# Cross-attention on one core: the second batch's queries from seven half-width products in place of eight

## The chip, the cores and the metric

The kernel runs on one core of a Trainium2 chip. Its engines work in parallel, each through its own list of instructions and in that list's order: TensorE (PE) multiplies matrices, VectorE (DVE) reduces, adds and transposes, ScalarE (ACT) copies and takes exponentials, GpSimd (POOL) does elementwise work, and SyncE (SP) issues nearly all DMAs. They meet at semaphores. The metric is device time in microseconds (us); lower is better. Three runs of the kernel before gave 497.66, 497.72 and 498.04 us, so its median is 497.72.

## The reference, cut to what matters

`x` is (2, 2048, 640), the context is (2, 154, 1024), all in f32; 20 heads of 32. The first 77 rows of the context are text, the other 77 are image prompts, each with its own keys, values and softmax.

```python
q    = split(x @ Wq.T)
k, v = split(text @ Wk.T), split(text @ Wv.T)
ki, vi = split(ip @ Wk_ip.T), split(ip @ Wv_ip.T)
out  = softmax(q k' / sqrt(32)) v + softmax(q ki' / sqrt(32)) vi
return merge(out) @ Wo.T + bo + x
```

## The kernel before, in words

Everything is transposed, with channels on the 128 partitions: 640 channels are 5 chunks of 128 (4 heads each), and the 2048 tokens of a batch are 4 blocks of 512. A *unit* `u` is half a batch's tokens (1024, two blocks `h`) of one chunk; there are 20 units, the first ten of batch 0. Two units make a chunk `q` of a batch (0 to 9).

Work on a unit: `queries` multiplies one token block by one chunk of Wq (5 matmuls of 512 columns, one per chunk of contracted channels), and `take_queries` copies the result out of PSUM, scaled by 1/sqrt(32). The unit's eight tiles of 128 tokens form three groups `s` of 3, 3 and 2 tiles. For each group `scores` (R) multiplies queries by keys into one *half* of PSUM, four banks of the eight, one bank per head; `take` (K, on ACT) copies the scores into the buffer `pb`; `maxima` (M, DVE); `subtract` (S, POOL); `exponential` (E, ACT); `sums` (D, DVE); `invert` (I, DVE); `normalise` (N, POOL); `transpose` (T, DVE). When both units of a chunk are through, `attend` (A, PE) multiplies by the values, and CA copies its result to `aT`.

Three tables of (unit, group) give other softmax forms. A BIASED group subtracts its maxima inside the exponential (one ACT instruction for each row of 77, so no S on POOL), a DIRECT group does so straight from PSUM (no K, and its banks stay taken until E is done), and a SUMMED group also lets ACT sum the rows (no D on DVE, and a read of the accumulator on ACT behind each exponential).

The output projection of batch 0 is done with seven block products in place of eight (`product`, m and cm in the list, with the token differences G of `sum_t` on POOL and the weight sums W). That of batch 1 is the tail of the kernel: weight sums V, token sums X, 66 products F and their sums Y into the output, with `last_chunk` for the fifth chunk (p, z, yz).

What sets the order is a list of words written out by hand or by a program, `SCHEDULE`. Each word emits one step, `@n` names its bank or half, and since every engine runs its own instructions in the order of emission, the list sets the order on all engines at once, SP's DMAs included: LX loads a token block of batch 1, LQ a chunk of Wq, VS spreads values, SF and SS fetch and store batch 0's output, and LA loads what batch 1's outputs are added to.

In batch 1, before the change, each (chunk, block) is loaded anew (20 LX words) into a ring of three blocks, and its queries are made by `queries`: 20 groups of 5 matmuls in this batch.

## Time and profile before

| what | value |
|---|---|
| median of three runs | 497.72 us |
| span of the profiled execution | 496.7 us |
| PE busy | 490.3 us (99%) |
| DVE busy | 408.5 us (82%) |
| POOL busy | 362.5 us (73%) |
| ACT busy | 315.0 us (63%) |
| bytes moved by DMA | 69.38 MB |
| granted TensorE clock | 1.000 |

A busy time is the time in which at least one instruction of the engine was under way. Matmuls overlap, so the mean duration of one (601 ns for 512 columns) is more than the distance from one to the next; the distance is read from the starts in the timeline. An f32 matmul of the source shows as two MATMUL records. The chain of waits follows the last instruction back to the first. The profiled execution's span is 1.0 us below the median of the runs.

### The profile page before, as it was taken

The page shows a single profiled execution, that of the slowest core. Times are in us where ns is not written, and L with a number is a line of the kernel's source. Part 1 is how long each engine was busy: PE and PEld are TensorE (multiplying, and loading weights), DVE is VectorE, ACT ScalarE, POOL GpSimd, SP SyncE. Part 2 cuts the span into 40 slices and gives each one's busy share as a digit, 9 for nine tenths or more (in the row PEclk, how much of TensorE's full clock was granted, in tenths as well). Part 3 has the DMA queues.
Part 4 walks back from the last instruction along what each step waited for, and adds up shares of the span by engine and source line. Part 5 has one row for each costly group of instructions (what it writes and reads, how often), then busy time and mean ns, then how long its engine had stood idle before and what let it go on. Part 6 is the DMA issues. An engine that isn't in the chain of part 4 may idle for free.

```text
span 496.7 us, 10482 instructions
## 1 busy us (share of the span) xinstructions
PE 490.3 (99%) x4114; PEld 287.9 (58%) x4114; DVE 408.5 (82%) x412; ACT 315.0 (63%) x1021; POOL 362.5 (73%) x157
## 2 busy tenths in 40 slices
PE   8999999999999999999999999999999999999997
PEld 5676657657547556456647654755755675444442
DVE  0069989979979989969976896687999978898877
ACT  1165878978978778668999786587578966100000
POOL 0069978798888999989874858565899888284830
PEclk9999999999999999999999999999999999999999
DMA  8991440332360454886445177418525401420115
GB/s 259 356 246 40 132 120 1 106 93 69 92 213 3 132 178 132 274 273 237 158 152 191 58 244 210 133 57 246 174 69 171 127 23 43 149 84 1 43 73 223
DMA packets 67474, 69.38 MB, mean 140 GB/s; under 512 B 5473, under 2 KB 47201, under 8 KB 67425
## 3 DMA queue, kind: packets, MB, share of 16 engines
q1 hardware_dynamic: 66704, 68.00, 43.8%
q8 instruction: 32, 0.52, 0.5%
q10 hardware_dynamic: 720, 0.72, 0.4%
q14 instruction: 18, 0.14, 0.1%
HBM read 54.94 MB, written 10.49 MB: 132 GB/s over the span
## 4 chain that ended last, share of the span: by engine, by line
PE 92%; DMA 3%; SPq 1%; DVE 1%; POOL 1%; ACT 1%; issue 0%; POOLq 0%
PE bank L201 33%; PE bank L848 11%; PE bank L490 10%; PE bank L233 10%; PE bank L332 10%; PE bank L142 9%; PE bank L471 6%; PE bank L500 3%; DMA aT<-in_L_xattn_Wk_ip_dram 2%; DMA wq<-in_L_xattn_Wq_dram 2%; SPq L534 1%; POOL pb L316 1%; DVE den L306 0%; ACT pb L301 0%; SPq L132 0%
## 5 line engine op out<-in xcount | busy, mean ns | idle before, releaser
L316 POOL TENSOR_TENSOR pb<-pb,rden 128x1848 f32<-128x1848 f32 (+1 forms) x60 | 176.1, 2944 | 39.7 <-DVE rden L311 35.5
L201 PE MATMUL bank<-x,wq 128*128 128x512 f32 x400 | 180.4, 601 | 0.6 <-DMA x<-in_x_dram 0.5
L295 POOL TENSOR_TENSOR pb<-pb,mx 128x1848 f32<-128x1848 f32 (+1 forms) x38 | 119.3, 3152 | 51.8 <-DVE mx L281 51.5
L201 PEld LDWEIGHTS bank<-x,wq 128*128 128x128 f32 x400 | 74.1, 191 | 86.7 <-issue 80.8
L323 DVE STREAM_TRANSPOSE pb<-pb 128x1920 f32<-128x1920 f32 (+1 forms) x60 | 115.7, 1932 | 4.9 <-POOL pb L316 4.3
L281 DVE TENSOR_REDUCE mx<-pb 128x24 f32<-128x1848 f32 (+1 forms) x51 | 93.7, 1850 | 30.7 <-ACT pb L245 30.5
L245 ACT COPY pb<-bank 128x462 f32<-128x462 f32 (+1 forms) x204 | 87.2, 539 | 36.0 <-PE bank L233 35.4
L306 DVE TENSOR_REDUCE den<-pb 128x24 f32<-128x1848 f32 (+1 forms) x47 | 88.7, 1895 | 17.6 <-ACT pb L301 13.3
L301 ACT ACTIVATE pb<-pb 128x1848 f32<-128x1848 f32 (+1 forms) x38 | 64.2, 1696 | 17.8 <-POOL pb L295 17.5
L269 ACT ACTIVATE pb<-pb,mx 128x77 f32<-128x77 f32 x224 | 67.8, 364 | 0.3 <-DVE mx L281 0.2
L233 PEld LDWEIGHTS bank<-kT,qT 32*128 32x128 f32 x1280 | 45.4, 184 | 26.9 <-issue 15.6
L269 ACT ACTIVATE pb<-bank,mx 128x77 f32<-128x77 f32 x184 | 51.8, 386 | 9.3 <-DVE mx L284 9.3
L233 PE MATMUL bank<-kT,qT 32*128 32x154 f32 x1280 | 56.2, 305 | 0.3 <-ACT kT L559 0.3
L332 PE MATMUL bank<-pb,v 32*32 32x512 f32 x1600 | 55.2, 597 | 0.0
L142 PE MATMUL bank<-wo_ct,aT 128*128 128x154 f32 x320 | 45.6, 296 | 0.3 <-DMA aT<-in_L_xattn_Wk_ip_dram 0.3
L142 PEld LDWEIGHTS bank<-wo_ct,aT 128*128 128x128 f32 x320 | 42.9, 188 | 3.6 <-issue 2.2
L332 PEld LDWEIGHTS bank<-pb,v 32*32 32x32 f32 x1600 | 29.9, 103 | 22.8 <-issue 10.7
L211 ACT ACTIVATE qT<-bank 128x512 f32<-128x512 f32 x40 | 24.2, 619 | 22.1 <-PE bank L201 22.0
L471 PE MATMUL bank<-aT,wo_ct 128*128 128x512 f32 x80 | 36.1, 596 | 0.0
L269 ACT ACTIVATION_READ_ACCUMULATOR pb<-bank,mx 128x1 f32 x128 | 33.6, 267 | 0.0
L490 PE MATMUL bank<-aT,wo_ct 128*128 128x256 f32 x128 | 32.3, 385 | 0.0
L490 PEld LDWEIGHTS bank<-aT,wo_ct 128*128 128x128 f32 x128 | 23.7, 190 | 6.5 <-issue 3.0
(75 smaller groups left out, 434.4 us busy)
## 6 DMA issues: line engine op xcount, KB each, us to landing
x<-in_x_dram SPq DMA_DIRECT2D x20, 1280.0 KB, 6.7
out_dram<-acc SPq DMA_DIRECT2D x20, 256.0 KB, 2.3
x<-in_x_dram SPq DMA_DIRECT2D x18, 256.0 KB, 5.9
acc<-in_x_dram SPq DMA_DIRECT2D x16, 256.0 KB, 4.7
out_dram<-x SPq DMA_DIRECT2D x15, 256.0 KB, 2.0
v<-vS SPq DMA_DIRECT2D x160, 20.0 KB, 2.8
wq<-in_L_xattn_Wq_dram SPq DMA_DIRECT2D x9, 320.0 KB, 5.0
aT<-in_L_xattn_Wk_dram SPq DMA_DIRECT2D x5, 512.0 KB, 5.5
```

Of the source, the lines that this page charges most:

```text
L142: nc.tensor.matmul(keys_in(out), loaded[n][:, k, :], cT[:, k, :, t, :], start=(k == 0), stop=(k == NCC - 1))
L201: nc.tensor.matmul(pq, wqs[q % 3][:, k, :], xs[place_of(u, h)][:, k, :], start=(k == 0), stop=(k == NC - 1),)
L233: nc.tensor.matmul(ps[g][:, ts(t, 2 * L)], qTs[(u, h)][g * D : (g + 1) * D, ts(st, P)], kT[g * D : (g + 1) * D, c, b].rearrange("p t l -> ...
L245: nc.scalar.copy(keys_of(u, s)[:, :, g], ps[g][:, : n * 2 * L].rearrange("p (n l) -> p n l", n=n))
L269: nc.scalar.activation(row, row if ps is None else rows_in(ps[g], n)[:, t, x], AF.Exp, bias=maxs[(u, s)][:, *one], accum_out=None if den i ...
L281: nc.vector.tensor_reduce(mx, rows_of(u, s), AX.X, ALU.max, negate=negate)
L295: nc.gpsimd.tensor_tensor(rows_of(u, s), rows_of(u, s), maxs[(u, s)].unsqueeze(3).to_broadcast([P, n, 2, L]), ALU.subtract)
L306: nc.vector.tensor_reduce(den_of(u, s), rows_of(u, s), AX.X, ALU.add)
L316: nc.gpsimd.tensor_tensor(rows_of(u, s), rows_of(u, s), rdens[(u, s)].unsqueeze(3).to_broadcast([P, n, 2, L]), ALU.mult)
L323: nc.vector.transpose(p, p)
L332: nc.tensor.matmul(pa[r][g * D : (g + 1) * D, :], v4s[q % 2][rows, g, k, :], zones[rows, :, g, k, :], start=(k == 0), stop=(k == NK - 1),)
L490: nc.tensor.matmul(part, w_of[m][:, kp, op], t_of(m, b, i)[:, kp], start=(op == kp == 0 and m in (1, 2, 5)), stop=(op == 1 and kp == 1 and ...
```

## The change

1. Batch 1's chunks are taken in pairs: chunks 0 and 1 (`p` = 0), 2 and 3 (`p` = 1). For each pair and each token block `i`, the first four channel chunks form a 2x2 block product: two output chunks by two pairs of input chunks, and two halves of 256 tokens. It is computed from seven products `q_product` (words g) of 2 matmuls of 256 columns; the fifth input chunk is added to four of them with one more matmul of 256 columns. `take_q_product` (words t) puts the results into the query tiles: products 1, 4, 5 and 6 by a copy on ACT, 2, 3 and 7 by an add or subtract on DVE. Product 6 goes on accumulating in the bank of product 1, then 7, then 4; product 3 goes on in that of 5.
2. The token sums (`sum_x`, words U, four per pair and block) are written into the token blocks themselves and one spare place; 24 are on POOL and 8 on DVE. The weight sums (`sum_wq`, words Z, six per pair) are on POOL.
3. Token blocks of batch 1 are loaded for a pair: 12 LX words, into a ring of two blocks (`RING`). The third block that batch 0 leaves (`SPARE`) holds two more query tiles, the spare token sum and the weight sums. LA now loads the output's tokens into it as well, ahead of the other two loads.
4. The scale 1/sqrt(32) moves from the queries to the keys. Query tiles come from a list kept by hand (`new_q`, `used_q`) in place of a pool.
5. The three tables of softmax forms are new: DIRECT has 7 groups in place of 9, BIASED 15 in place of 13, SUMMED 8 in place of 13. Groups that need S on POOL are still 38, of which 12 in place of 5 are groups of two tiles.
6. SCHEDULE is written anew.

```diff
-        (11, 0), (13, 0), (13, 2), (14, 0), (14, 2), (15, 1), (15, 2), (16, 2), (18, 1),
+        (3, 2), (7, 1), (11, 0), (11, 2), (13, 0), (13, 2), (15, 1),
...
-    qpool = ctx.enter_context(tc.tile_pool(name="qpool", bufs=5))
+    q_slots = [const.tile([P, TB], F32, name=f"qs_{n}") for n in range(QS)]
...
-        return late.index((u, h)) % XROOM if b else sub * NH + h
+        return late.index((first_of(u), h)) % RING if b else sub * NH + h
...
-        nc.scalar.mul(qT, pq, SCALE)
+        nc.scalar.copy(new_q(u, h), pq)
...
+    def sum_x(p, i, n, eng):
+        x, y = {
+            1: lambda: (x_part(p, i, 0, 0), x_part(p, i, 0, 1)),
+            2: lambda: (x_sum(p, i, 1), x_part(p, i, 1, 1)),
+            3: lambda: (x_part(p, i, 0, 1), x_part(p, i, 1, 1)),
+            4: lambda: (x_sum(p, i, 2), x_part(p, i, 1, 0)),
+        }[n]()
+        eng.tensor_tensor(x_sum(p, i, n), x, y, ALU.add)
...
+    def q_product(p, i, m, ps):
+        w = {
+            1: lambda: wq_part(p, 0, 0), 2: lambda: wq_part(p, 0, 1), 4: lambda: wq_part(p, 1, 1),
+        }.get(m, lambda: wq_sum(p, m))()
...
+        part = ps[:, :HT]
+        for kp in range(2):
+            nc.tensor.matmul(
+                part, w[:, kp], x[:, kp], start=(kp == 0 and m in (1, 2, 5)), stop=(kp == 1 and not fifth),
+                skip_group_check=True,
+            )
+        if fifth:
...
+            nc.tensor.matmul(part, w5, five, start=False, stop=True, skip_group_check=True)
+    def take_q_product(p, i, m, ps):
...
+        if m in (2, 3, 7):
+            nc.vector.tensor_tensor(t, t, ps[:, :HT], ALU.add if m == 2 else ALU.subtract)
+        elif half:
+            nc.scalar.mul(t, ps[:, :HT], -1.0)
+        else:
+            nc.scalar.copy(t, ps[:, :HT])
...
-            nc.scalar.copy(kT[:, 0, b, t, :], keys_in(ps)[:, b])
+            nc.scalar.mul(kT[:, 0, b, t, :], keys_in(ps)[:, b], SCALE)
...
-        "R0.0@1 R1.0@0 K0.0 q.1.0@4 LK.5 K1.0 M0.0 M1.0 S0.0 R2.0@0 v.0.0@6 K2.0 cq.1.0 S1.0 M2.0 E0.0 v.0.1@0 LK.6 "
+        "R2.0@0 K2.0 R0.0@1 K0.0 M2.0 R1.0@0 K1.0 q.1.0@5 cq.1.0 M0.0 S2.0 LK.4 M1.0 S0.0 E0.0 D0.0 q.1.1@2 E2.0 S1.0 "
...
+        elif k == "U":
+            sum_x(x, y, int(args[2]), nc.vector if args[3] == "d" else nc.gpsimd)
+        elif k == "Z":
+            sum_wq(x, y, nc.vector if args[2] == "d" else nc.gpsimd)
+        elif k == "g":
+            m = int(args[2])
+            at[name] = banks[int(where)] if where else at[f"g.{x}.{y}.{({6: 1, 7: 1, 4: 1, 3: 5})[m]}"]
+            q_product(x, y, m, at[name])
+        elif k == "t":
+            take_q_product(x, y, int(args[2]), at["g" + name[1:]])
...
+            home[third] = xs[SPARE]
+            nc.sync.dma_start(
+                out=xs[SPARE], in_=xT[:, ds(S + third * TB, TB)].rearrange("(k p) t -> p k t", p=P)
+            )
```

How the order changes is shown at three places.

First, PE at the opening: the scores (L233 before, L259 now) of unit 0 and the query product behind them. Names: `qT_0`, `qs_84` and `qs_85` are query tiles; banks 71 to 74 and 67 to 70 before are the two halves of PSUM, now 68 to 71 and 64 to 67. Before:

```order
L233 MATMUL bank_71<-kT,qT_0_146 128x154 [waits Activation_49]
L233 MATMUL bank_72<-kT,qT_0_146 128x154
L233 MATMUL bank_67<-kT,qT_0_146 128x154
L233 MATMUL bank_68<-kT,qT_0_146 128x154
L201 MATMUL bank_71<-x_84,wq_75 128x512 [waits DMAHW4_49,Activation_49]
L233 MATMUL bank_67<-kT,qT_1_153 128x154 [waits Activation_49]
```

Now:

```order
L259 MATMUL bank_64<-kT,qs_85 128x154 [waits Activation_49]
L259 MATMUL bank_65<-kT,qs_85 128x154
L259 MATMUL bank_68<-kT,qs_84 128x154
L259 MATMUL bank_69<-kT,qs_84 128x154
L259 MATMUL bank_64<-kT,qs_84 128x154 [waits Activation_49]
L259 MATMUL bank_65<-kT,qs_84 128x154 [waits Activation_49]
L229 MATMUL bank_69<-x_81,wq_72 128x512 [waits DMAHW4_49,Activation_49]
```

The two-tile group moved ahead of the two others, so that the third group writes the half that the first has just filled, and stands ahead of the query product, which stood between them.

Second, PE behind chunk 3's attention (batch 1's first queries). `x_79`, `x_80` are the two token blocks of the ring, `x_81` the spare block with sums of weights and tokens, `wq_*` chunks of Wq. Before, three query groups in a row:

```order
L201 MATMUL bank_67<-x_83,wq_77 128x512 x5
L201 MATMUL bank_69<-x_84,wq_77 128x512 x5
L201 MATMUL bank_70<-x_82,wq_77 128x512 x5
L233 MATMUL bank_71<-kT,qT_0_1610 128x154
L233 MATMUL bank_72<-kT,qT_0_1610 128x154
```

Now:

```order
L617 MATMUL bank_68<-x_80,x_81 128x256 x2
L617 MATMUL bank_65<-x_81 128x256 x2
L624 MATMUL bank_65<-x_80,x_81 128x256
L617 MATMUL bank_66<-x_80,wq_74 128x256 x2
L624 MATMUL bank_66<-x_80,wq_74 128x256
L617 MATMUL bank_68<-x_80,wq_72 128x256 x2
L617 MATMUL bank_69<-x_79,wq_74 128x256 x2
L143 MATMUL bank_70<-wo_ct,aT 128x154 x8
```

Bank 68 takes product 6 and, two products later, product 7 of the same block, which waits until ACT has copied product 6 out.

Third, POOL from chunk 3's attention on. L295, L322 are `subtract`, L316, L343 `normalise`, L570 `sum_x`, L594 and L595 a weight sum. Before:

```order
L316 TENSOR_TENSOR pb<-pb,rden_1_1490 128x12x154
L295 TENSOR_TENSOR pb<-pb,mx_2_1494 128x8x154
L295 TENSOR_TENSOR pb<-pb,mx_0_1508 128x12x154
L295 TENSOR_TENSOR pb<-pb,mx_1_1526 128x12x154
L316 TENSOR_TENSOR pb<-pb,rden_0_1619 128x12x154
L316 TENSOR_TENSOR pb<-pb,rden_1_1666 128x12x154
```

Now:

```order
L343 TENSOR_TENSOR pb<-pb,rden_2_1499 128x8x154
L570 TENSOR_TENSOR x_79<-x_79 128x2x256
L594 TENSOR_TENSOR x_81<-wq_72,wq_74 128x256
L595 TENSOR_TENSOR x_81<-x_81,wq_72 128x256
L322 TENSOR_TENSOR pb<-pb,mx_1_1537 128x12x154
L322 TENSOR_TENSOR pb<-pb,mx_2_1565 128x8x154
L570 TENSOR_TENSOR x_81<-x_80 128x512
L570 TENSOR_TENSOR x_80<-x_80 128x2x256
L343 TENSOR_TENSOR pb<-pb,rden_0_1668 128x12x154
```

Sums of tokens and weights stand between the softmax steps, where before only softmax steps stood.

More of the change, by code (lines that the diff above doesn't have):

```diff
@@ L177, with first_of @@
     XROOM = NHB - 1
+    SPARE = RING
+    def first_of(u):
+        q, b, c, sub = step_of(u)
+        return u - SUB if b and c % 2 else u
     def place_of(u, h):
         _, b, _, sub = step_of(u)
-        return late.index((u, h)) % XROOM if b else sub * NH + h
+        return late.index((first_of(u), h)) % RING if b else sub * NH + h
     def load_block(u, h):
@@ L188, in load_block, with new_q, used_q @@
         )
+    spare = xs[SPARE].rearrange("p k t -> p (k t)")
+    q_more = [spare[:, ts(n, TB)] for n in range(2)]
+    x_first = spare[:, ds(2 * TB, TB)].rearrange("p (k t) -> p k t", k=2)
+    wq_room = spare[:, ds(3 * TB, 8 * P)].rearrange("p (k o) -> p k o", o=P)
+    q_uses, q_idle, q_late = {}, list(q_slots), list(q_more)
+    def new_q(u, h):
+        if u >= NU // 2 and q_late:
+            q_idle[:0] = q_late
+            q_late.clear()
+        t = q_idle.pop(0)
+        qTs[(u, h)], q_uses[(u, h)] = t, NT // NH
+        return t
+    def used_q(u, h):
+        q_uses[(u, h)] -= 1
+        if not q_uses[(u, h)]:
+            q_idle.append(qTs[(u, h)])
     def load_wq(q):
@@ new lines, in take_q_product @@
+    def take_q_product(p, i, m, ps):
+        h = i % NH
+        o, half = {1: (0, 0), 2: (0, 0), 6: (0, 1), 3: (0, 1), 5: (1, 1), 7: (1, 1), 4: (1, 0)}[m]
+        u = unit_of(p, i)[0] + SUB * o
+        t = (qTs[(u, h)] if (u, h) in qTs else new_q(u, h))[:, ts(half, HT)]
+        if m in (2, 3, 7):
+            nc.vector.tensor_tensor(t, t, ps[:, :HT], ALU.add if m == 2 else ALU.subtract)
+        elif half:
+            nc.scalar.mul(t, ps[:, :HT], -1.0)
+        else:
+            nc.scalar.copy(t, ps[:, :HT])
@@ L809, in finish @@
         elif k == "LA":
-            for u, h in late[-XROOM:]:
+            for u, h in late[-RING:]:
                 home[step_of(u)[3] * NH + h] = xs[place_of(u, h)]
-            (fourth,) = set(range(NHB)) - set(home)
+            third, fourth = sorted(set(range(NHB)) - set(home))
+            home[third] = xs[SPARE]
+            nc.sync.dma_start(
+                out=xs[SPARE], in_=xT[:, ds(S + third * TB, TB)].rearrange("(k p) t -> p k t", p=P)
+            )
             nc.sync.dma_start(
```

51 lines of the change are left out of this document (44 added, 7 removed), and 131 rows, old and new, of the table SCHEDULE.

## The prediction

> **What bounds the kernel now.** I read the page's totals first, then the chain of waits, then PE's timeline.
>
> ```profile
> span 496.7 us, 10482 instructions
> PE 490.3 (99%) x4114; PEld 287.9 (58%) x4114; DVE 408.5 (82%) x412; ACT 315.0 (63%) x1021; POOL 362.5 (73%) x157
> ...
> PE 92%; DMA 3%; SPq 1%; DVE 1%; POOL 1%; ACT 1%; issue 0%; POOLq 0%
> ```
>
> PE is busy 99% of the span, and 92% of the chain that ended last is PE's own work. Overlapping matmuls could make a busy PE look fuller than it is, so the distance between starts decides:
>
> ```profile
> 414.52 3.17 PE L471 MATMUL bank<-aT,wo_ct 128*128 128x512 f32 x7
> 417.53 1.03 PE L490 MATMUL bank<-aT,wo_ct 128*128 128x256 f32 x4
> 418.39 0.59 PE L500 MATMUL bank<-aT,wo_ct 128*128 128x256 f32 x2
> 418.82 1.03 PE L490 MATMUL bank<-aT,wo_ct 128*128 128x256 f32 x4
> 419.69 0.59 PE L500 MATMUL bank<-aT,wo_ct 128*128 128x256 f32 x2
> 420.12 3.60 PE L471 MATMUL bank<-aT,wo_ct 128*128 128x512 f32 x8
> ```
>
> Seven records of 512 columns take 417.53 - 414.52 = 3.01 us, 0.430 each. Twelve of 256 columns take 420.12 - 417.53 = 2.59 us, 0.216 each. Half the columns cost half the time and there is no gap between shapes. So PE runs at its own pace, and what PE no longer has to do comes off the time, as long as the others keep up. Both are stated per record; a matmul of the source is two, so 0.860 and 0.432.
>
> How near the others are is read from stretches of the trace, here the one from chunk 3's attention to chunk 6's, the one from chunk 7's to chunk 8's, and the tail:
>
> ```profile
> core 0: us, PE busy (x) PEld busy (x) DVE busy (x) ACT busy (x) POOL busy (x), PEclk, DMA share, GB/s
> 179.00:301.20 122.20, 122.03 (x1146) 71.64 (x1147) 106.75 (x105) 102.40 (x391) 98.36 (x40) 1.00 0.58 188
> 346.20:388.70 42.50, 42.50 (x397) 26.19 (x400) 40.36 (x38) 31.58 (x100) 38.64 (x17) 1.00 0.45 139
> 423.60:496.70 73.10, 69.39 (x309) 30.69 (x308) 59.83 (x93) 2.31 (x8) 32.76 (x20) 1.00 0.25 92
> ```
>
> With PE full, DVE stood at 95% and POOL at 91% in the busiest of these (40.36 and 38.64 of 42.50). The clock is 1.00 throughout.
>
> **The change part by part.** *Matmuls.* 16 of batch 1's 20 query groups go, 80 matmuls of 512 columns: 80 x 0.860 = 68.8 us. In come 56 products of two matmuls and 32 matmuls for the fifth chunk, 144 of 256 columns: 144 x 0.432 = 62.2 us. PE saves 6.6 us. Seven for eight would be an eighth of the 55 us that is not the fifth chunk, 6.9 us; the rest is rounding of the two paces.
>
> *Switches of PE's mode.* Scores and attention use parts of the array, everything else all of it.
>
> ```profile
> 35.85 4.45 PE L201 MATMUL bank<-x,wq 128*128 128x512 f32 x10
> 40.23 1.85 PE L233 MATMUL bank<-kT,qT 32*128 32x154 f32 x48
> 42.01 2.38 PE L142 MATMUL bank<-wo_ct,aT 128*128 128x154 f32 x16
> ...
> 64.29 1.07 PE L233 MATMUL bank<-kT,qT 32*128 32x154 f32 x24
> 65.29 4.56 PE L201 MATMUL bank<-x,wq 128*128 128x512 f32 x10
> 69.78 0.76 PE L332 MATMUL bank<-pb,v 32*32 32x512 f32 x12
> ```
>
> Going in costs 4.38 - 4.30 = 0.08 us at 35.85 and 4.49 - 4.30 = 0.19 at 65.29. Coming out: 48 scores take 1.78 us and 24 take 1.00, so 24 cost 0.78 and the exit 0.22. In PE's order, runs on the whole array go from 51 to 55 and runs of scores from 46 to 48, which is 4 more ways in and 3 more ways out: 4 x 0.08 to 0.19 plus 3 x 0.22 = 1.0 to 1.4 us, taken as 1.2.
>
> *The opening.* The third group of scores now writes the half that the first group filled, so PE waits until ACT has copied that out.
>
> ```profile
> 24.41 1.96 PE L233 MATMUL bank<-kT,qT 32*128 32x154 f32 x48 [0.31 <-ACT kT L559]
> 26.30 4.56 PE L201 MATMUL bank<-x,wq 128*128 128x512 f32 x10
> ...
> 25.50 3.68 ACT L245 COPY pb<-bank 128x462 f32<-128x462 f32 x8 [1.01 <-PE bank L233]
> 31.61 1.38 ACT L245 COPY pb<-bank 128x308 f32<-128x308 f32 x4 [2.43 <-PE bank L233]
> ```
>
> Before, the query product at 26.30 came in with no gap. Now: 32 scores take 0.52 us, to 24.93; ACT starts some 0.3 later (25.50 stands 0.3 behind the first 24 scores' 24.41 + 0.78) and copies for 1.38, to 26.6; the third group needs 0.78 + 0.22, to 27.6. Without the wait the three groups would end at 24.41 + 2.08 + 0.22 = 26.7. PE loses 0.9 us here. Bounds: 0, if the copies of two tiles free the banks one by one as fast as PE asks, and 1.4, a whole copy.
>
> *ACT.* 16 copies of query tiles go, 32 copies of half a tile come; S groups become smaller, and elements with their own exponential rise from 408 to 464 while accumulator reads fall from 248 to 176.
>
> ```profile
> L211 ACT ACTIVATE qT<-bank 128x512 f32<-128x512 f32 x40 | 24.2, 619 | 22.1 <-PE bank L201 22.0
> L359 ACT COPY aT<-bank 128x256 f32<-128x256 f32 x40 | 11.4, 404 | 12.1 <-POOL pb L828 10.8 <-PE bank L332 1.3
> L269 ACT ACTIVATE pb<-pb,mx 128x77 f32<-128x77 f32 x224 | 67.8, 364 | 0.3 <-DVE mx L281 0.2
> ```
>
> 16 x 0.619 = 9.9 against 32 x 0.404 = 12.9, and 56 elements at 67.8 / 224 = 0.30 add 17 before the 72 reads saved. ACT gains some 10 us on 315, 66% of the new span, off the path. The scale moved to the keys changes no count and costs nothing.
>
> *DVE and POOL.* Rows that price them:
>
> ```profile
> L316 POOL TENSOR_TENSOR pb<-pb,rden 128x1848 f32<-128x1848 f32 x40 | 131.3, 3288 | 24.8 <-DVE rden L311 22.7 <-ACT aT L355 1.1 <-ACT pb L245 0.6
> L295 POOL TENSOR_TENSOR pb<-pb,mx 128x1232 f32<-128x1232 f32 x5 | 11.3, 2253 | 0.0
> L431 POOL TENSOR_TENSOR aT<-aT 128x512 f32<-128x512 f32 x8 | 10.2, 1278 | 0.1
> L401 POOL TENSOR_TENSOR x<-wo_ct 128x256 f32<-128x256 f32 x1 | 0.7, 736 | 0.0
> L306 DVE TENSOR_REDUCE den<-pb 128x16 f32<-128x1232 f32 x12 | 16.9, 1412 | 3.6 <-ACT pb L269 3.6
> L515 DVE SCALAR_TENSOR_TENSOR acc<-bank,bo_sb,acc 128x256 f32<-128x256 f32 x32 | 13.7, 468 | 7.0 <-PE bank L500 7.0
> L834 DVE TENSOR_TENSOR pb<-aT 128x1024 f32<-128x1024 f32 x7 | 8.3, 1221 | 1.7 <-PE bank L332 1.5 <-ACT aT L359 0.2
> ```
>
> POOL: subtract loses seven groups of 3.29 us and gains seven of 2.25 (-7.2); 24 token sums at 1.28 (+30.7); twelve half-tile weight operations at 0.74 and four smaller ones, some 0.5 each (+10.9). That is +34, to 397 us, 81%. DVE: six more small sums and one large one fewer (+6.5), 24 takes at 0.47 at most (+11), eight token sums at half of 1.22 (+4.9): about +21, to 430, 87%.
>
> Most of it lands between chunk 3's attention and chunk 6's, where 48 of the 56 products stand. Counted there: POOL had 9 large and 1 small subtract, 12 and 7 normalises, 5 token differences and the output's weight sums, 99 us by the rows (the trace: 98.4). It gets 5 and 3 subtracts, 12 and 6 normalises, 6 differences, the same weight sums, 21 token sums and 7 words Z: 122 us. PE's own work there goes from 122.2 to about 124. DVE goes from 106.8 to about 119. So in this stretch POOL needs 98% of PE's time and DVE 96%. The cover that hid POOL (24 us of idle) is used up. Some 41 us of POOL's 122 (token sums, Z, differences) wait for no softmax step and can fill the gaps between those that do, so I charge little: 0.9 us. Below nothing is excluded, since no work leaves POOL or DVE there; the upper bound is POOL at the 91% that the trace has shown beside a full PE: 122 / 0.91 = 134 us, 10 us over PE.
>
> *Eight token sums on DVE.* Two operands in SBUF, while POOL reads SBUF nearly all the time. The trace shows what such a meeting does:
>
> ```profile
> 436.31 1.22 DVE L834 TENSOR_TENSOR pb<-aT 128x1024 f32<-128x1024 f32 x1
> 436.48 1.37 POOL L828 TENSOR_TENSOR pb<-wo_ct,pb 128x128 f32<-128x128 f32 x1 [7.57 <-DVE pb L828]
> 459.58 0.46 POOL L828 TENSOR_TENSOR pb<-pb,wo_ct 128x128 f32<-128x128 f32 x1 [6.66 <-DVE pb L828]
> ```
>
> POOL's operation took 1.37 us in place of 0.46 and ended 0.3 us behind DVE's sum: it stood still until that was done. Now it is mostly DVE that would come second, behind an operation of up to 3.29 us. A wait of 0 to 3.29 each, seven times in the stretch, is 0 to 23 us of DVE's time there, of which 5 are slack. The Trainium skill, "SBUF — State Buffer", section "Who interferes with whom", says that a DVE instruction with two SBUF inputs and a GpSimd instruction that reads SBUF exclude each other for a whole instruction, the first to start winning; by it a sum can wait out a whole subtract or normalise, which is the last of the rivals but one; the trace agrees (1.37 us against 0.46). I take no wait beyond the 0.9 above, since each of these sums follows a token sum on POOL, at whose end POOL is between operations.
>
> *DMAs and the tail.* Eight loads of 1.28 MB go. LA's new load goes ahead of the two others:
>
> ```profile
> x<-in_x_dram SPq DMA_DIRECT2D x20, 1280.0 KB, 6.7
> ```
>
> The first takes 6.7 us to land and the other two, 1.3 MB together, nearly as long again, so the last lands some 12 us behind LA's issue, and DVE's first output sum (yz of that block) can start only 10.6 us behind attention anyway (5.45 of attention, 0.86 for one F, 3.43 + 0.86 of last_chunk). DVE may wait 1 to 2 us there, out of 73.1 - 59.8 = 13 of slack. Cost 0; 2 if the slack cannot be used.
>
> *Sum.* Against the profiled execution: 496.7 - 6.6 + 1.2 + 0.9 + 0.9 = 493.1 us of span. The median stands 1.0 above (497.72 against 496.7): **494.1 us**, 0.7% faster.
>
> **The rivals.**
> *PE gets all of it (492.1).* The opening overlaps and nothing new stalls: 497.7 - 6.6 + 1.0 = 492.1. For it: PE was busy for all but 0.2 us of the stretch where most changes. Against it: three engines at 96 to 100% in one stretch.
> *All of it goes to POOL (496.7 to 498.7).* POOL reaches 95% between chunk 3 and chunk 6: 122 / 0.95 = 128.5, which is 4.5 over PE's 124 where I took 0.9: 497.7, no change.
> *POOL sets the pace there (503).* POOL stays at the 91% of the trace: 134 against 124, PE waits 10 us, 494.1 + 9 = 503. Place: chunk 3's attention to chunk 6's; mechanism: a normalise that waits for DVE's reciprocal leaves POOL idle, token sums come late, ACT's exponentials and with them the copies t behind them come late, and a product that goes on in the same bank waits. It decides from a POOL share under 95%. For it: no stretch so far shows more than 91%. Against: there PE and not POOL set the pace.
> *The eight sums block DVE (505).* At 2.5 us each DVE needs 119 + 7 x 2.5 = 136.5 for 124 of PE: 12 us, of which I have counted 0.9, so 505. Against the time before it decides from 128.5 = 119 + 7 x 1.4, 1.4 us each.
> *The change doesn't do what it says* is excluded as far as PE goes: 256 columns do cost half.
>
> **How the numbers follow.** A measurement of this kernel can tell about 0.2%, that is 1 us, from no change. Chances: my forecast 0.54 (492.5 to 496.7), PE gets all 0.15 (below 492.5), all to POOL 0.13 (496.7 to 498.7), POOL sets the pace 0.13 and blocked sums 0.05 (both above 498.7). So faster 0.69, within 0.2% 0.13, slower 0.18. The range for 8 in 10 goes from 490.5, which takes in the gaining side but for some 0.04, to 499.5, which leaves out 0.16. The forecast's own range is 492.5 to 496.7.
>
> **What would show it.** L201's successor has 240 records and the products 288, 0.216 us apart; if they stand further apart, the first term is wrong. PE shows a gap of about 1 us near 26 us. From chunk 3's attention to chunk 6's, POOL's share is over 95% and PE has no wait over 1 us; if PE's weight loads there wait for ACT's copies t, or a token sum on DVE lasts 2 us and more, a rival has won. The tail from the last attention takes 73 us as before; over 75 would mean that LA's loads come late.

## The result, and the profile after

The changed kernel takes 501.22 us (median of six runs, 500.91 to 503.3) against 497.69 before (six runs, 497.52 to 498.04): a ratio of 1.0075, 95% interval 1.0062 to 1.0088. It is slower by 0.75% where 0.7% faster was predicted.

From the page of the changed kernel, the totals and the chain of waits by engine:

```profile
span 499.4 us, 10833 instructions
...
PE 489.5 (98%) x4242; PEld 313.7 (63%) x4242; DVE 431.3 (86%) x443; ACT 324.2 (65%) x1029; POOL 398.6 (80%) x197
...
PE 70%; DVE 9%; ACT 8%; POOL 7%; DMA 2%; issue 2%; SPq 1%; ACTq 0%; DVEq 0%; POOLq 0%
```

The counted loads came as counted: POOL 398.6 us (397 predicted), DVE 431.3 (430), ACT 324.2 (325). What changed is the chain: PE's own work is 70% of it, where it was 92%.

PE's timeline, from one product to the next:

```profile
204.40 1.02 PE L617 MATMUL bank<-x,x 128*128 128x256 f32 x4
...
209.15 1.03 PE L617 MATMUL bank<-x 128*128 128x256 f32 x4
```

Between the first and the last start lie 22 records (4+2+4+2+4+2+4) in 4.75 us, 0.216 each, as before. So the products cost what was worked out, and the loss is waiting. For both profiled executions I took the distances between the starts of PE's records, less the pace of each shape (0.4295 us for 512 columns, 0.216 for 256, 0.132 for 154, 0.0324 for a score, 0.0307 in attention) and less the usual price of a switch of PE's mode (0.19 into scores or attention, 0.22 out of scores, 0.54 out of attention); what is left is waits, in us:

| stage (to the start of an attention) | before | after | difference |
|---|---|---|---|
| start to chunk 0 | 3.43 | 4.17 | +0.74 |
| chunk 0 to 2 | 0.45 | 0.66 | +0.21 |
| chunk 2 to 3 | 0.23 | 0.92 | +0.69 |
| chunk 3 to 4 | 0.17 | 2.38 | +2.21 |
| chunk 4 to 5 | 0.25 | 3.03 | +2.78 |
| chunk 5 to 6 | 0.26 | 0.06 | -0.20 |
| chunk 6 to 9 | 0.93 | 1.66 | +0.73 |
| last attention to the end (whole length) | 73.1 | 73.9 | +0.8 |

That is +8.0; the switches come to 26.2 in place of 25.0, which is 1.2 more, and the matmuls to 6.5 less, so the span should grow by 2.7, and it grew by 2.7. The profiled execution of before was not a typical one: in later runs of the same kernel the span was mostly 495.4 to 496.5 and the time 1.8 above it, as in the changed kernel (501.2 against 499.4). So 0.8 us of the loss shows only against the usual span. Where the shown execution of before spent it is not known; it may be at the start, since the first scores begin at 24.4 us in both executions shown here, and in most kernels below between 23.1 and 24.0.

The stretch from chunk 3's attention to chunk 6's, in its three stages and as a whole, and the tail (windows; columns as in the prediction):

```profile
182.30:225.30 43.00, 41.38 (x435) 32.80 (x434) 39.17 (x39) 38.00 (x120) 40.33 (x21) 1.00 0.42 130
225.30:266.60 41.30, 40.97 (x407) 30.19 (x408) 38.00 (x44) 37.56 (x163) 41.06 (x28) 1.00 0.32 103
266.60:311.70 45.10, 45.10 (x433) 34.42 (x432) 42.36 (x48) 38.64 (x142) 41.01 (x21) 1.00 0.36 111
sum 129.40, PE 127.45 PEld 97.40 DVE 119.53 ACT 114.21 POOL 122.41; mean PE 42.48 PEld 32.47 DVE 39.84 ACT 38.07 POOL 40.80
...
425.50:499.40 73.90, 69.62 (x308) 30.62 (x308) 61.96 (x95) 2.31 (x8) 39.02 (x28) 0.99 0.31 112
```

Between the attention of chunks 4 and 5 POOL is busy for 41.06 of 41.30 us: it has no gap left. PE still shows 40.97, but a busy PE includes matmuls that stand waiting. Four places in these two stages show how. At 195.4, 210.5 and 241.5 us PE's timeline has (some rows of ACT between them):

```profile
194.57 1.83 ACT L328 ACTIVATE pb<-pb 128x1848 f32<-128x1848 f32 x1
196.38 0.48 ACT L637 COPY qs<-bank 128x256 f32<-128x256 f32 x1
196.91 1.13 PE L617 MATMUL bank<-x,x 128*128 128x256 f32 x4 [0.48 <-ACT qs L637]
...
211.72 0.64 ACT L635 ACTIVATE qs<-bank 128x256 f32<-128x256 f32 x2
212.41 1.13 PE L617 MATMUL bank<-x,x 128*128 128x256 f32 x4 [0.80 <-ACT qs L635]
...
242.61 3.17 ACT L272 COPY pb<-bank 128x462 f32<-128x462 f32 x8
242.79 0.81 PE L259 MATMUL bank<-kT,qs 32*128 32x154 f32 x16 [0.20 <-DVE acc L542]
243.41 1.92 PE L259 MATMUL bank<-kT,x 32*128 32x154 f32 x16
245.27 1.13 PE L617 MATMUL bank<-x,wq 128*128 128x256 f32 x4
```

The product at 196.91 goes on in a bank that ACT has just emptied with the copy at 196.38, and that copy stood behind an exponential. At 212.41 it is the same behind 24 exponentials of one row block each. At 241.5 three score groups follow each other; the third (243.41, 16 records in 1.92 us where 0.52 is the pace) writes the half that the first filled, and waits for the copies at 242.61. These three are 0.55, 0.87 and 1.70 us over PE's pace.

The fourth place is at 232.3 us, behind chunk 4's attention:

```profile
230.25 1.23 ACT L328 ACTIVATE pb<-pb 128x1232 f32<-128x1232 f32 x1 [0.85 <-POOL pb L322]
231.39 2.03 ACT L382 COPY aT<-bank 128x512 f32<-128x512 f32 x4
232.29 2.22 PE L259 MATMUL bank<-kT,qs 32*128 32x154 f32 x24
```

ACT's exponential waits 0.85 us for a subtraction on POOL, the four copies of the attention's result stand behind it, and the scores that are written into the same banks wait for the copies: 1.16 us over PE's pace. The four places make 4.3 of the 5.4 us of waits in these two stages.

And the chain of waits, in order of time, for the stage from chunk 4 to 5:

```profile
223.42 6.00 ACT pb L296 x24
...
229.44 2.08 DVE den L333
...
233.88 3.24 POOL pb L343
...
240.62 1.23 POOL x L570
241.85 2.21 POOL pb L343
...
250.02 2.37 POOL x L428 x2
...
257.85 1.24 POOL aT L458
259.09 0.04 issue
259.13 1.99 PE bank L517 x8
```

From 233.4 to 259.1 the chain is POOL: normalises, the second pair's weight sums (between them), a token sum (L570), the output's weight sums (L428), until PE's product at 259.1 is released by a token difference (L458). PE itself loses only 0.15 us there: POOL's queue ends just as late as PE, which has lost its time at 232.3 and 241.5 by then.

### The profile page after: what moved, and what is told of

It reads as the page before. It is cut to its first block, busy times and chain, and to the rows that moved or that the text cites. A ratio compares the mean times of both kernels' runs of the same rounds, so it can differ in the third digit from the quotient of the medians.

```text
span 499.4 us, 10833 instructions
## 1 busy us (share of the span) xinstructions
PE 489.5 (98%) x4242; PEld 313.7 (63%) x4242; DVE 431.3 (86%) x443; ACT 324.2 (65%) x1029; POOL 398.6 (80%) x197
## 4 chain that ended last, share of the span: by engine, by line
PE 70%; DVE 9%; ACT 8%; POOL 7%; DMA 2%; issue 2%; SPq 1%; ACTq 0%; DVEq 0%; POOLq 0%
PE bank L229 18%; PE bank L259 9%; PE bank L617 9%; PE bank L143 8%; PE bank L359 8%; PE bank L984 7%; PE bank L517 6%; ACT pb L296 4%; POOL pb L343 3%; PE bank L624 2%; PE bank L498 2%; ACT pb L272 2%; DMA aT<-in_L_xattn_Wk_ip_dram 2%; DVE pb L964 2%; DVE pb L970 1%
## 5 line engine op out<-in xcount | busy, mean ns | idle before, releaser
L343 POOL TENSOR_TENSOR pb<-pb,rden 128x1848 f32<-128x1848 f32 (+1 forms) x60 | 176.6, 2955 | 16.2 <-DVE rden L338 15.8
L322 POOL TENSOR_TENSOR pb<-pb,mx 128x1848 f32<-128x1848 f32 (+1 forms) x38 | 112.6, 2970 | 44.7 <-DVE mx L308 44.7
L229 PE MATMUL bank<-x,wq 128*128 128x512 f32 x240 | 109.1, 604 | 0.5 <-DMA x<-in_x_dram 0.3
L333 DVE TENSOR_REDUCE den<-pb 128x24 f32<-128x1848 f32 (+1 forms) x52 | 94.9, 1828 | 12.4 <-ACT pb L328 7.2
L296 ACT ACTIVATE pb<-pb,mx 128x77 f32<-128x77 f32 x320 | 87.9, 365 | 1.3 <-DVE mx L308 1.3
L229 PEld LDWEIGHTS bank<-x,wq 128*128 128x128 f32 x240 | 44.5, 192 | 51.9 <-issue 46.4
L259 PEld LDWEIGHTS bank<-kT,qs 32*128 32x128 f32 x1024 | 38.0, 184 | 22.0 <-issue 14.3
L259 PE MATMUL bank<-kT,qs 32*128 32x154 f32 x1024 | 48.9, 308 | 0.9 <-issue 0.4
L296 ACT ACTIVATE pb<-bank,mx 128x77 f32<-128x77 f32 x144 | 40.8, 390 | 1.2 <-DVE mx L311 1.2
L617 PE MATMUL bank<-x,wq 128*128 128x256 f32 x128 | 33.6, 388 | 0.2
L570 POOL TENSOR_TENSOR x<-x 128x512 f32<-128x512 f32 x24 | 31.8, 1333 | 1.9 <-DMA x<-in_x_dram 1.0
```

The lines of the kernel that those rows point to most:

```text
L229: nc.tensor.matmul(pq, wqs[q % 3][:, k, :], xs[place_of(u, h)][:, k, :], start=(k == 0), stop=(k == NC - 1),)
L259: nc.tensor.matmul(ps[g][:, ts(t, 2 * L)], qTs[(u, h)][g * D : (g + 1) * D, ts(st, P)], kT[g * D : (g + 1) * D, c, b].rearrange("p t l -> ...
L296: nc.scalar.activation(row, row if ps is None else rows_in(ps[g], n)[:, t, x], AF.Exp, bias=maxs[(u, s)][:, *one], accum_out=None if den i ...
L322: nc.gpsimd.tensor_tensor(rows_of(u, s), rows_of(u, s), maxs[(u, s)].unsqueeze(3).to_broadcast([P, n, 2, L]), ALU.subtract)
L333: nc.vector.tensor_reduce(den_of(u, s), rows_of(u, s), AX.X, ALU.add)
L343: nc.gpsimd.tensor_tensor(rows_of(u, s), rows_of(u, s), rdens[(u, s)].unsqueeze(3).to_broadcast([P, n, 2, L]), ALU.mult)
```

## The experiments

Eighteen kernels ran, each beside runs of the kernel before (medians 497.46 to 497.71). Times are medians; a pair in brackets is the 95% interval of the ratio to before. The theories, as they came up, with their names in the expectations: the added load of POOL (1, later D); copies late in ACT's queue (2, later A); the eight sums on DVE (3); the new order and the new softmax forms (B); refills of TensorE's instructions (C); DVE's load (E); single copies between groups that share banks (F).

**The sums.** In `sum_x`, 16 of 512 columns, for all 32 sums or for DVE's eight:

```diff
-        eng.tensor_tensor(x_sum(p, i, n), x, y, ALU.add)
+        eng.tensor_tensor(x_sum(p, i, n)[:, :, :8], x[:, :, :8], y[:, :, :8], ALU.add)
```

> All 32 token sums U keep their place and their waits, but work on 16 of 512 columns (so the queries of batch 1 are wrong: most of the sums is left out). POOL loses 24 x some 1.2 us, DVE 8 x some 0.5 us and its meetings with POOL. Theory 1, POOL sets the pace from chunk 3's attention to chunk 6's (122.4 us busy of 129.4): the stretch falls from 129.4 to 124 or 125 us and the time to 495.5 to 496.5. Theory 2, the copies t on ACT and the products that go on in one bank set it (order and latency, not load): the stretch stays above 128 and the time at 500 to 501. Theory 3, the eight sums on DVE and POOL's operations that shut each other out: the stretch falls as in theory 1, but so it does when only DVE's eight are cut.

> Only the 8 token sums on DVE are cut to 16 of 512 columns (queries wrong: most of these eight sums is left out); the 24 on POOL are whole. Theory 1 (POOL's load): POOL keeps its 122 us less some 2 us of operations that no longer stretch, so 499 to 500. Theory 3 (mutual exclusion): nearly all of the five us in the stretch come back, 496.5 or less. Theory 2: 500.5 to 501.

All sums cut: 499.34 us, 1.0039 (1.0022 to 1.0055). DVE's alone: 501.29, 1.0085 (1.0065 to 1.0104). So 28 us off POOL (370.8 in place of 398.6) and 2 off DVE win 1.9 us, and DVE's sums nothing. They do meet POOL's operations, as the prediction feared, but rarely for long:

```profile
L570 DVE TENSOR_TENSOR x<-x,x x8: 628/734/1699, 176.9 to 298.9; 128x512 f32<-128x512 f32 x8
```

Least, median and longest: one of eight took 1.7 us, some 2 us are lost in all.

**POOL loaded more.** The eight sums to POOL (`U....d` to `U....p` in the order); and two groups, (9, 1) and (10, 0), out of BIASED, with their `S` behind their `M`:

> The 8 token sums of DVE are moved to POOL, the kernel computes everything. Theory 1 (POOL's load): 7 x 1.23 = 8.6 us more on POOL in the stretch from chunk 3 to chunk 6, less 2.4 us of stretched operations: 6 us longer, 506 to 508. Theory 3 (mutual exclusion): no meetings are left, 498 to 500. Theory 2: 501 to 503.

> The changed kernel complete, with the exponentials of two groups (chunk 9's second, chunk 10's first) in the plain form: 8.7 us less on ScalarE, two subtractions of 3.3 us more on GpSimd, all between the attention of chunks 3 and 4. Theory A: the waits at 210.5 and 232.3 us go, 499.5. Theory D: GpSimd has 6.6 us more where it is said to set the pace, 504 to 507.

508.69 (1.0227, 1.02 to 1.0254) and 515.13 (1.0354, 1.0335 to 1.0374). Seven us more on POOL (405.6) cost 7.5 us, and 6.5 more (405.1), all of it within one stage, cost 14, more than theory D had. Not all of that is waiting for POOL: in sums_on_pool the granted clock was 0.50 or 0.51 in three stretches of 3.4 us (from 152.5, 183.3 and 241.3 us), which is an estimated 5 us of lost pace, and the first of them stands behind a pause that has nothing to do with POOL (the refill, below). The stage from chunk 3 to 4 of plain_forms, and PE's longest waits in it:

```profile
182.20:240.20 58.00, 44.20 (x443) 34.47 (x446) 44.61 (x40) 33.88 (x90) 48.74 (x25) 0.91 0.34 104
```

```profile
PE bank L617 <- POOL x L570: 7.3, 1, 7.3
PE bank L617 <- DVE qs L633: 3.0, 2, 1.9
```

PE waits 7.3 us at one place for a token sum that stands in POOL's queue, and the granted clock is 0.91 in the stage. ACT's relief (316.2 us in place of 324.2) bought nothing.

**ACT and DVE relieved, alone and together.**

```diff
 def exponential_of(u, s, ps=None, den=None):
+        if den is None and 9 <= u <= 14:
+            if ps is None:
+                exponential(u, s)
+            else: ...one activation per bank
+            return
 def sums(u, s):
+        rows = rows_of(u, s)[:, :, :, :8] if 9 <= u <= 14 else rows_of(u, s)
```

> ScalarE alone is relieved where the extra waits lie: in chunks 9 to 14 each softmax group that takes its exponentials in 16 or 24 instructions with the row's maximum as a bias, and no sums (eight groups, about 30 us of ScalarE in all, 20 of them before the attention of chunk 6), takes them in one instruction (four out of the banks); the subtraction of the maximum is left out there. GpSimd's and VectorE's work is the same. Theory A (TensorE waits for copies that stand in ScalarE's queue behind these exponentials): the 7.1 us of waits between the attention of chunks 3 and 6 fall to 3.5 or less, 497 to 498. Theory D (GpSimd's 122 us in 129 set the pace): no change, 501.

> VectorE alone is relieved: in chunks 9 to 14 the row sums of the exponentials read 8 of 77 columns (15 groups, about 1.7 us less each, some 22 us of it between the attention of chunks 3 and 6). Theory E (VectorE's load is the rest of the waits): 129.4 us from the attention of chunk 3 to that of 6 fall to 127 or less, 498 to 499. Theory F (the rest are places of the order, where TensorE waits for one copy): 501, the waits of 1.7 us at 241.5 and 0.55 at 195.4 in place.

> The same, and the 32 sums of token blocks cut to 16 of their 512 columns, which relieves GpSimd by 28 us and VectorE by 4. If the two causes add: what light_act gains and the 1.9 us of the cut sums, about 495.5. If ScalarE's queue was all there is in the stretch: as light_act. If whichever of the two is left sets the pace: clearly less than the two gains together, under 495.

> All three engines relieved at once: eight groups' exponentials in one instruction each without the maximum, all token sums cut to 16 of 512 columns, row sums over 8 of 77 columns in chunks 9 to 14. TensorE's own work from the attention of chunk 3 to that of 6 is 122.3 us; light_both took 127.2. Theory E: 124.5 or less. Theory F: 126.5 or more, with the waits of 1.7 us and 0.55 still there.

light_act, with 27 us less on ACT, 501.36 (1.0057 to 1.0094): nothing. light_dve 502.21 (1.0066 to 1.011): nothing. light_both 499.08 (1.0021 to 1.0046) and light_all 499.19 (1.0025 to 1.005): what small_sums gave. Theories A and E fall as theories of load. The totals also move by 1 or 2 us with the refill's pause ahead of chunk 3's attention (below), so the stretch from chunk 3 to 6 is the better measure: 129.4 us in the changed kernel, 129.5 in light_act, 130.0 in light_dve, 128.1 in small_sums, 127.4 in light_both and 127.8 in light_all, one profiled execution each. The stage from chunk 4 to 5 again, of light_act, small_sums and light_all:

```profile
225.90:267.10 41.20, 40.91 (x402) 30.15 (x402) 37.86 (x44) 31.64 (x127) 40.97 (x28) 1.00 0.31 98
```

```profile
224.90:265.30 40.40, 40.36 (x405) 29.73 (x404) 36.27 (x44) 37.66 (x164) 36.05 (x28) 1.00 0.34 106
```

```profile
223.70:263.90 40.20, 40.16 (x403) 29.79 (x402) 31.19 (x44) 31.76 (x127) 35.98 (x28) 1.00 0.34 107
```

With ACT lighter POOL is still full and the stage is as long. With POOL lighter (36 us) it falls by only 1 us, most of it at 232.3, where the wait goes from 1.16 to 0.44 us. With all three light it stays there: 40.2, still 2.0 over PE's own 38.2 (41.2 less 3.03), with the 1.70 us of the three score groups in place.

**Single copies made short.** In `take`, chunks 9 to 14 copy 8 of 154 columns per tile:

> In chunks 9 to 14 the copies of the scores out of the banks take 8 of 154 columns per tile: each of the four copies of a group some 0.25 us in place of 0.5, the group's four 1.0 in place of 1.9; the rest of the scores is left as it lay. Theory F (TensorE waits for single copies between groups that use the same banks): the wait of 1.7 us at 241.5 falls under 1.0 and that of 0.55 at 195.4 goes, 127 to 128 us in place of 129.4 between the attention of chunks 3 and 6, 499 to 500. If the copies' time is not it: 129.4 and 501.

501.34 (1.0046 to 1.0097); in the profiled execution, the fastest of four at 499.92, 128.4 us from 3 to 6. The two places that theory F named behave as it says: the wait at 195.4 goes, that of 1.70 falls to 0.48. But PE then stands elsewhere:

```profile
240.66 0.70 PE L259 MATMUL bank<-kT,x 32*128 32x154 f32 x16
241.55 0.81 PE L259 MATMUL bank<-kT,qs 32*128 32x154 f32 x16 [0.19 <-DVE acc L543]
242.18 0.70 PE L259 MATMUL bank<-kT,x 32*128 32x154 f32 x16
...
255.69 1.07 PE L259 MATMUL bank<-kT,qs 32*128 32x154 f32 x24
256.56 1.27 POOL L459 TENSOR_TENSOR aT<-aT,x 128x512 f32<-128x512 f32 x1
257.88 1.35 PE L518 MATMUL bank<-aT,x 128*128 128x256 f32 x5 [1.13 <-POOL aT L459]
```

At 257.88 it waits 1.13 us for POOL's token difference, the one of the chain above, 33.8 us behind chunk 4's attention (224.1) as in the changed kernel (259.1 less 225.3). The stage is 41.2 again: POOL sets it once the copies don't.

**The order alone.** Four moves, no work less:

```diff
-K0.9 R2.9@0 K2.9 ... E1.8 D1.8 v.4.0@5 cv.4.0 LK.19 t.0.1.1 R1.9@0
+K0.9 R2.9@0 K2.9 ... t.0.1.1 E1.8 D1.8 v.4.0@5 cv.4.0 LK.19 R1.9@0
-A.4@1 E2.10 g.0.3.4 S1.10 CA.4
+A.4@1 CA.4 E2.10 g.0.3.4 S1.10
-K1.11 Z.1.3.p R2.12@1 R2.11@0 K2.12 G5.0 M1.11 g.1.0.1@5 M2.11 ... g.1.0.5@4
+R2.12@1 K2.12 K1.11 Z.1.3.p G5.0 M1.11 g.1.0.1@5 ... g.1.0.5@4 R2.11@0 M2.11
```

> The changed kernel complete, with four moves in the order and no work less: the copy of the product that TensorE waits for at 195.4 us goes ahead of an exponential on ScalarE, the attention's copies at 231.4 go ahead of an exponential, and of the three score groups in a row at 241.5 the third goes behind two products, with the copies of the second taken first. Theory A: waits of 0.55, 0.6 and about 0.7 us go: 499.4. Theory D: no change, 501.2. If the order elsewhere was fitted to these places: new waits behind them, 501 or more.

505.19 (1.0132 to 1.0166): 4 us lost. The product at 195.8 no longer waited for its first copy, but the next product waited 0.75 for another; the attention's copies came 0.8 earlier, and then the second of the three score groups waited 1.6 us for DVE, whose work had not moved. Behind that wait the granted clock was 0.60 from 244.9 to 246.5 and 0.50 to 248.2, an estimated 1.5 of the 4 us. Every wait taken away came back at the next place.

**The products undone in the new order.** Plain query groups at places of the products, sums and Z gone:

```diff
-g.0.0.1@3 t.0.0.1 ... g.0.0.6 t.0.0.6 g.0.0.5@1 ... g.0.0.7 ... (7 products, 4 sums)
+q.10.0@3 cq.10.0 ... q.12.0@3 cq.12.0
```

> Only the products are undone: both pairs of query groups by the eight plain products again, no sums and no copies t; the new order of everything else and the new softmax forms stay. TensorE has 6.6 - 1.2 = 5.4 us more work of its own than in the changed kernel (501.2). Theory A (the waits between chunks 3 and 6 come from the products' own copies on ScalarE and sums on GpSimd): about 5 us of these waits go, so 501.2 + 5.4 - 5 = 501.6, and the stalls over TensorE's pace between the attention of chunks 3 and 6 return to about 2.4 us. Theory B (the waits come from the new order and the new softmax forms, whatever the products are): they stay, 506 to 507.

> The products of the first pair alone are undone: TensorE has 2.7 us more work than in the changed kernel, up to the attention of chunk 4. Theory A: the 3.3 us of extra waits between the attention of chunks 2 and 4 go, those between 4 and 5 stay: 500.5. Theory B: 503.9. If it were GpSimd's load as a whole rather than what stands in ScalarE's queue at a place, the waits after chunk 4 would shrink too: under 500.

> The products of the second pair alone are undone: TensorE has 2.7 us more work, after the attention of chunk 4. Theory A: the 2.7 us of extra waits between the attention of chunks 4 and 5 go, those before stay: about 501.2. Theory B: 503.9. GpSimd's load as a whole: the waits before chunk 4 stay and about 2 us go after it, near 501.9.

530.87 (1.0651 to 1.0683), 513.55 (1.0299 to 1.0349; three of four runs, the other took 521.59) and 519.75 (1.0395 to 1.0487): far beyond either theory. In eight_both, with POOL at 28.8 us of 52.6 from chunk 3 to 4, ACT's queue stands still for whole query groups (16 us in six waits, 4.3 the longest):

```profile
ACT qs L238 <- PE bank L229: 16.0, 6, 4.3
```

Behind these waits stand the copies of scores that PE needs. So the new order is fitted to small products spread between the score groups; it cannot be priced apart from them, and these three don't tell A from B. What they do show is which waits are not the products': eight_both, which has none, keeps a pause inside a score group at 150.7 us (0.94 from one score to the next; below), takes 35.96 us from chunk 8's attention to chunk 9's (35.95 in the changed kernel, 34.99 before) and 73.9 in the tail.

**The opening, and TensorE's instructions.** The first words as before the change (three-tile groups first); 32 matmuls of one column after the warm-up; both ideas together, with 12 such matmuls:

```diff
-R2.0@0 K2.0 R0.0@1 K0.0 M2.0 R1.0@0 K1.0 q.1.0@5 ...
+R0.0@1 K0.0 R1.0@0 K1.0 q.1.0@5 M0.0 M1.0 S0.0 LK.4 R2.0@0 ...
+    for _ in range(12):
+        nc.tensor.matmul(banks[0][:D, :1], warm[:, :D], warm[:, :1], start=True, stop=True)
```

> Only the first words change: the groups of three tiles go first again, the query product stands between the second and third group, and a value product behind the next one. The wait of the third group on ACT's copies is gone. If the 0.7 us that the first attention comes later (70.5 against 69.8) is this wait and nothing later absorbs it: 500.3 to 500.7. If a later engine sets the pace anyway: 501.1 to 501.3.

> The changed kernel with 32 more matmuls of one column after the warm-up ones, before any data has come: nothing that follows is altered but where TensorE's instructions lie against the 16,384-byte refills of its instruction queue. Theory C (the gap of 0.7 us inside a score group at 150.8 us is TensorE waiting for a refill): the gap moves or goes, 500.3 to 500.6 if no other refill falls badly. If the gap is a wait on data or on a bank: 501.2, gap in place.

> The changed kernel complete, with the opening's three-tile score groups first as before and 12 matmuls of one column between the first queries and the first keys, where TensorE waits for weights (the 32 of shift32 took 0.1 us each). Theory C (a refill of TensorE's instructions falls into a score group near 150 us, and nothing but their place decides it): the stage from the attention of chunk 2 to that of 3 takes 36.0 us as in shift32 in place of 37.0 to 39.8, and with the opening's 0.9 us the run is at 499.3. If 12 matmuls don't move the refill out of the score group: as opening, 500.3 or more.

opening 500.9 (1.0054 to 1.0094; two of four runs at 500.3 and 500.4, not clear of the changed kernel's 500.9 to 503.3), shift32 504.31 (1.0089 to 1.0184), opening_shift 499.83 (1.003 to 1.0062). PE's instructions come in refills of some 16 KB on queue q8 (0.54 MB in 33): 33 in the changed kernel, 32 before, 34 in shift32, which is about PE's matmuls and weight loads (8,484, 8,228 and 8,612) by 256. From the first scores to the first attention opening takes 45.94 us, the changed kernel 46.12 and the kernel before 45.37: the old first words bring back 0.2 of the 0.75. At 150.8 us of the changed kernel PE pauses inside a score group, for nothing that the profile names, and a refill has gone out between 149 and 150 while the DMA engines are full of loads:

```profile
150.76 0.79 PE L259 MATMUL bank<-kT,qs 32*128 32x154 f32 x13
151.94 0.79 PE L259 MATMUL bank<-kT,qs 32*128 32x154 f32 x11 [0.39 <-issue]
```

```profile
q1 hardware_dynamic: 216, 0.39, 102.3%
q8 instruction: 1, 0.02, 6.5%
```

In opening_shift the refill goes out between 146 and 147 us, where the loads take 32.4%, and the group runs through:

```profile
150.39 1.07 PE L259 MATMUL bank<-kT,qs 32*128 32x154 f32 x24
151.39 1.85 PE L143 MATMUL bank<-wo_ct,aT 128*128 128x154 f32 x12
```

From chunk 2's attention to chunk 3's it takes 36.1 us and so does shift32, against 37.0 in the changed kernel and 36.9 to 39.8 in the others that keep all seven products (43.6 in sums_on_pool, where PE waits for POOL too).

That the pause is a wait for instructions shows in all 17 profiled kernels without the extra matmuls: it stands behind the same 13th record of this score group, whatever the time, and PE goes on 2.4 to 2.7 us after a refill's packet has gone out (149.4 and 151.9 in the changed kernel, 148.4 and 150.9 in light_all, 150.1 and 152.7 in old_tail). So far theory C holds. That the loads made this refill late is not shown: its packet took 1.04 us, that of opening_shift 1.29, and a refill at 131.9 us goes out among loads at 116% without a pause behind it.

Shift32 paid with its opening: its 32 matmuls took 3.4 us ahead of the first queries, and its first attention came 4 us later. Opening_shift, 0.46% slower than the kernel before, is the best complete version with the seven products.

The Trainium skill, "Runtime: NRT & Kernel Launch", section "Instruction fetch mechanics", says that the cost of crossing a boundary of 16 KB is mostly hidden. The changed kernel's trace agrees for the other 32 refills, behind which PE shows no pause of its own over 0.5 us; this one cost 0.7 us, and up to 2.1 in the other kernels.

**The tail.** `old_tail` puts the kernel before's order back behind the last attention; `tuned` adds the opening and `CA.4` ahead of `E2.10`.

> The changed kernel complete; behind the last attention the words stand in the kernel before's order again (three sums of weights that were already done there excepted). If the new order of the tail's additions costs its 0.85 us: the tail takes 73.1 in place of 73.9 and the run 500.4. If it is something else that arrives late: 501.2.

> Three moves of the order together, kernel complete: the opening's three-tile score groups first as before (0.9), the attention's copies ahead of an exponential at 231.4 (0.85 were won there by act_order, before it lost more elsewhere), the old order of the tail (0.85). If these waits are independent: 501.2 - 2.6 = 498.6, still not under the kernel before. If each returns at the next place that waits: 500 to 501.

504.44 (1.0104 to 1.0154) and 504.96 (1.0132 to 1.0173). Both lost. The tail grew to 75.1 us: some weight sums of the old order now stand at its head, and PE waits 1.33 us at 446.4 for one of DVE's additions. So what makes the tail's 0.8 stays open. In `tuned` the attention's copies came earlier and the second score group of the three waited 1.6 us for DVE, as in act_order. Most of both losses lies elsewhere: from chunk 2 to 3 these executions take 39.8 and 39.7 us in place of 37.0, with a longer pause at the refill and the clock at half behind it (see the end).

## Why the prediction was wrong

- *Matmuls, -6.6:* right; 0.216 per record and the counts as stated. *Switches, +1.2:* right, 26.2 against 25.0.
- *Opening, +0.9:* right: the three groups take 27.61 - 24.38 = 3.23 us in place of 2.08 + 0.22, 0.93 more, of which 0.74 is left at the first attention. `opening` gave only 0.2 of it back.
- *Eight sums on DVE, 0:* right in effect. The rival with blocked sums is out. (Two sums in the prediction are off: DVE's three terms add up to 22.4, not 21, and 119 + 7 x 1.4 is 128.8, not 128.5. Nothing hangs on either.)
- *The stretch from chunk 3 to 6, +0.9:* this is the step that failed. It measured +4.8 (2.21 + 2.78 - 0.20). The load was right (122 and 119 us), and so were two of the signs by which I said a rival would have won: POOL's share came out at 94.6%, under the 95%, and PE's weight loads wait for ACT's copies t (0.71 us at 196.91). The step took load for the only cost. It said that 41 us of POOL's work "wait for no softmax step and can fill the gaps". From chunk 4 to 5 they did fill the gaps, to 99.4%, and that left POOL no room to be early: a subtraction comes late, ACT's exponential and the attention's copies behind it too, and PE loses 1.16 us at 232.3 (0.44 with the sums cut). I had averaged over three stages, of which the last has slack (41.0 of 45.1). The rival "POOL sets the pace" had part of the mechanism and the place; its price of 9 us over the forecast was too high, since PE waited 5, not 10.
- But POOL is only one of two limits there. With 28 us less on POOL the stage lost 1 us, to 40.4, and no relief of ACT and DVE took it lower than 40.2. Below POOL's limit lie waits for single copies between score groups and products in the same banks. I priced such a wait at the opening (one group behind a copy in its own half) and did not look for the same pattern elsewhere; the trace after has it at 195.4, 210.5 and 241.5, 3.1 us in all. With those copies shortened two of the waits went or shrank, and in the stage from chunk 4 to 5 PE waited for POOL instead. That both reliefs together would win the whole 4.8 is argued, not shown; it was not tried.
- *Not in the sum at all:* the refill's pause, 0.7 us (gone in shift32 and opening_shift), 0.7 between chunks 6 and 9 (PE waits 0.59 us for DVE's addition L548 at 408.5 and 0.4 for a transpose ahead of chunk 9's attention) and 0.8 in the tail, where DVE and POOL have 62.0 and 39.0 us in place of 59.8 and 32.8. None of these is the products' own: eight_both, without products, has the same pause, the same stage ahead of chunk 9 and the same tail. They belong to the new order or the new softmax forms; which of the two, no run here shows. I took a new order for free wherever no row of the loads spoke against it.
- *Tail and LA's loads, 0:* the loads were not late; most of the 0.8 is a wait of 0.53 us at 456.8 for one of DVE's additions (L926); why that comes later than before, no run shows.
- *The base:* 0.8 us, since the profiled execution of before was slower than its usual runs and I took 1.0 for what lies outside the span where 1.8 is usual.

The miss adds up: 8.0 of waits less the 1.8 foreseen, 6.2, and 0.8 of the base make 7.0, against 501.2 - 494.1 = 7.1.

## What to carry to other kernels

When work moves from a full engine to others that then run above 90%, take the load stage by stage, not over the whole stretch: a stage in which one queue has no gap left can't get shorter than that queue, and what other engines wait for in it comes late. When the order is written anew, scan it for pairs that share banks with a copy between them and less work between than that copy takes, and price each; here they stood just under the other limit, so that relieving one alone won 1 us or nothing in that stage. A gain of 5 us out of 500 is gone when ten such places cost half a microsecond each. And where runs differ by a pause that the edit doesn't touch, compare the stage that it does touch, not the total.

## What the runs showed of the hardware

- A refill of TensorE's instructions can stop TensorE in the middle of a score group: 0.7 us in the changed kernel, up to 2.1 in others, and nothing where it goes out 3 us earlier. In 17 traces TensorE went on 2.4 to 2.7 us after the refill's packet had gone out. Twelve idle matmuls moved it; what makes it late is open.
- A pause of that size can cost twice. In the profiled execution of `opening` it was longer, and the granted clock fell behind it (windows across it and behind it: mean clock 1.00, then 0.65):

```profile
149.30:151.70 2.40, 0.89 (x23) 0.57 (x14) 2.22 (x3) 2.15 (x5) 2.40 (x2) 1.00 1.03 368
151.70:155.20 3.50, 3.47 (x23) 3.31 (x23) 1.23 (x2) 1.89 (x4) 3.50 (x2) 0.65 0.22 68
```

The Trainium skill, "TensorE: Matmul & The Clock Gate", section "Part 1: The HAM clock gate", has the clock halved after an idle window of about 3.4 us. Here PE stood for only 1.54 us by the row of the pause, and the clock fell all the same, to 0.50 from 152.8 to 156.2:

```profile
151.73 0.79 PE L259 MATMUL bank<-kT,qs 32*128 32x154 f32 x11 [1.54 <-issue]
```

The length of the pause alone does not decide it: in light_act PE's row shows the same 1.54 us at 152.39, and the clock stayed at 1.00. A lower clock is the second reason why kernels that make PE wait long lose more than the waits: 0.91 over the 58 us of plain_forms' stage is an estimated 5 us.
